# Who issues the store of a scan unit's step sizes and input maps, and when its first broadcast is loaded

## The chip, the cores and the metric

The kernel runs on one core of a Trainium2 chip. Time is device time of that core, in microseconds (us), from one launch to the end. The kernel before was run three times: 4187.68 us in the median (4182.67 to 4189.44). The engines are named PE (matrix multiply), DVE (vector), ACT (scalar, activations), POOL (GpSimd) and SP (which here only issues transfers).

## What is computed

Four layers in sequence work on x of shape (4, 512, 256). Layers 0, 1 and 3 are attention and feed-forward layers. The change lies in layer 2, a stack of four selective-scan blocks (Mamba blocks). Cut to what matters, one block is:

```
xi, z = split(rmsnorm(h) @ in_proj.T)
xi = silu(conv(xi) + conv_b)
dt, Bm, Cm = split(xi @ x_proj.T)                 # 16, 16 and 16 columns
dt = softplus(dt @ dt_proj.T + dt_b)
dA = exp(dt[..., None] * A)
dBu = dt[..., None] * Bm[:, :, None, :] * xi[..., None]
h_t = dA_t * h_(t-1) + dBu_t                      # a scan over time
y_t = sum_s(h_t * Cm_t) + xi * D
h = h + (y * silu(z)) @ out_proj.T
```

There are 512 inner features, 16 states for each of them, and 512 time steps after a prefix of 64 that is scanned earlier, beside layers 0 and 1.

## The kernel before

Layer 2 is cut into 16 units: 4 blocks times 4 batch elements, in that order. Inner features lie on partitions, in four chunks of 128; time lies along the free dimension. A unit is 32 steps: two pairs of chunks, and in each pair 8 pairs of states times 2 chunks. One step is a scan over 128 partitions of two states of 512 time steps each, 1024 elements in a row. The steps of all units are numbered through: step i belongs to unit i // 32.

A step runs over these instructions, each with its own tile rotation:

- `maps` (L1581): for every second step, SP loads two rows of B (tile bB, 3 buffers) and two rows of C (bC, 4 buffers) from a scratch tensor in DRAM, copied to all 128 partitions (512 KB each). The loads are issued four or five steps ahead.
- `decay` (L1596): ACT writes exp(dt * A) for the two states into PSUM (ps_dA, 2 buffers), one step ahead, so the tile of step i + 2 can be made once step i has been read.
- `product` (L1588): POOL multiplies dt * xi (dtx) with bB into dBu (4 buffers), two steps ahead in program order.
- `begin` (L1606): ACT puts the start value of the two scans into the first column of dBu.
- `states` (L1611): DVE runs the scan. In steps with i % 4 == 1 it writes to the tile hP in SBUF, in the others back to ps_dA.
- `outputs_here` (L1623) on DVE, or `outputs` (L1628) on POOL for the hP steps, multiply the states with bC: the output multiply.
- `add_up` (L1632): PE transposes and sums the result into ps_y, for all 16 states of a pair.

The rest of a unit is written as generators that are advanced twice a step, in a fixed order, until they give back control with `yield`. Every yield is therefore half a step. `front` (L1325) prepares the unit after next: the norm of h (hn), its projection (ps_in, copied to xp by ACT), the convolution as four matmuls (ps_cv, made xi by ACT), a Silu over all of xi (issued at fixed steps of the running unit), and then, on ACT, the tile xd (L1428) with the 16 step-size rows and the 32 rows of B and C. xd is stored to two scratch tensors in DRAM: scr0, the first column of B, and scr, all of B and C. Then the first column is loaded back as b0, on all partitions. `step` (L1444) waits for the mark "fronted" that front sets at its end, and makes dt and dtx of a pair of chunks: a matmul of xd with w_dt (ps_dt), an Identity activation with bias for each chunk (L1459), softplus over both (L1266), products, and the start values from b0. The Sqrt of the unit after that (L1366) is timed to follow softplus in the same half step, since each change of function table on ACT is an ACT_TABLE_LOAD. `close_pair` (L1662) and `gated` (L1506) take the sum of a finished pair (g, DVE) through the gate and the output projection.

Two things set the order around the change. The instructions of each engine stand in the order in which the program emits them, and each engine takes its own in that order. SP's queue holds the stores of xd (L1432, L1433), the load of b0 (L1439), the map loads (L1585) and the weight loads, in one sequence.

Of the kernel before, what the change touches and what calls it, by code (L numbers as in the profile page):

```python
# [29 lines left out]
NS = 16  # L30
R = 16
# [93 lines left out]
def kernel(ctx: ExitStack, tc: tile.TileContext, t: dict, out: bass.AP):  # L125
    nc = tc.nc
# [1141 lines left out]
    def layer2(hT, A, far, h63, tail, X, fw, wl, late):  # L1268
# [5 lines left out]
        with ExitStack() as st:  # L1274
# [50 lines left out]
            def front(n):  # L1325
# [101 lines left out]
                xd = q["xd"] = pool.tile([NX, T], F32, name="xd", tag="xd")  # L1427
                nc.scalar.copy(xd, ps[:NX, :])  # L1428
                done(ps)
                scr = q["scr"] = dram.tile([2, NS, T], F32, name="scr", tag="scr")  # L1430
                scr0 = dram.tile([NS, 1], F32, name="scr0", tag="scr0")
                nc.sync.dma_start(out=scr0, in_=xd[R : R + NS, 0:1])  # L1432
                nc.sync.dma_start(out=scr.rearrange("k s t -> (k s) t"), in_=xd[R:, :])  # L1433
                for _ in range(3):
                    yield
                while n and units[n - 1].get("used0") != EC:
                    yield
# [252 lines left out]
            with tc.manual_schedule():  # L1690
                for i in range(first, last):
                    n, r = divmod(i, US)
# [8 lines left out]
                    if i in (first, first + 8) or 0 <= n < NU - 2 and r == FS:  # L1701
                        active.append(front(0 if i == first else 1 if i < 0 else n + 2))
# [243 lines left out]
```

## Time and profile before

| | us |
|---|---|
| median of 3 runs | 4187.68 |
| lowest and highest | 4182.67, 4189.44 |
| profiled execution, its own time | 4180.73 |
| span of the profiled execution | 4178.8 |
| layer 2's scan steps, first to last scan | 1645.6 to 3450.7 |
| store of xd by SP, first and last | 1622.1 and 3267.7 |
| transfers bB and bC, issue to landing, median | 4.2 and 3.9 |
| store scr0 and store scr, issue to landing, median | 1.3 and 3.1 |
| load b0, issue to landing, median | 7.1 |

Busy time over the whole span is PE 3496.8, DVE 2992.9, POOL 2359.9 and ACT 2222.6 us. In the page's row of slices (40 equal parts of the span, each digit the busy tenths), the scan block is the stretch where DVE stands at 9:

```profile
PE   7998988988898797777888888888887667999789
...
DVE  5537456466545622999999999999999996766653
ACT  2345465455312724666666666666666553556332
POOL 2249259076100503989888988899988881000131
```

A line of the trace gives the start in us, the duration, the engine and the line of the program, the operation with its tiles, and in brackets how long the engine stood idle before it and which instruction's end is taken to have released it. "SPq" is SP's queue: the duration there is that of the issue, not of the transfer. A row of waits gives who waited for whom, the total in us, how often, and the longest. A wait for several instructions is put down to the one that came last.

### The profile page before, as it was taken

How to read it: one execution, taken by the hardware profiler on the slowest of the kernel's cores; microseconds unless marked ns; L12 is line 12 of the kernel's file. 1: busy time of each engine (PE TensorE's matmuls, PEld its weight loads, DVE VectorE, ACT ScalarE, POOL GpSimd, SP SyncE). 2: the span in 40 equal slices, each digit the busy share in tenths (PEclk: the TensorE clock that was granted, in tenths of full speed). 3: DMA queues.
4: the chain of work that ended last, by engine and by line, in shares of the span. 5: the costliest groups of instructions: out<-in, count | busy, mean ns of one | idle time of the engine just before them, and what ended most of it. 6: DMA issues, size and time to landing. Idle time of an engine off the chain costs nothing. (4 is left out here: it accounts for less than half of the span.)

```text
span 4178.8 us, 48666 instructions
## 1 busy us (share of the span) xinstructions
PE 3496.8 (84%) x17616; PEld 2207.9 (53%) x17616; DVE 2992.9 (72%) x2853; ACT 2222.6 (53%) x4475; POOL 2359.9 (56%) x1601
## 2 busy tenths in 40 slices
PE   7998988988898797777888888888887667999789
PEld 4654544545566363555555555555555444555446
DVE  5537456466545622999999999999999996766653
ACT  2345465455312724666666666666666553556332
POOL 2249259076100503989888988899988881000131
PEclk9999999999998898889888888888888778999999
DMA  2023022023100202444444444444444441000000
GB/s 75 11 85 102 23 79 94 17 95 94 42 1 1 77 7 78 162 152 158 148 161 152 150 156 159 150 143 151 167 159 140 149 141 36 1 1 1 1 6 16
DMA packets 140287, 369.93 MB, mean 89 GB/s; under 512 B 20624, under 2 KB 38224, under 8 KB 140048
## 3 DMA queue, kind: packets, MB, share of 16 engines
q1 hardware_dynamic: 137968, 364.63, 25.9%
q8 instruction: 139, 2.28, 0.2%
q10 hardware_dynamic: 2080, 2.20, 0.2%
q14 instruction: 100, 0.82, 0.1%
HBM read 363.50 MB, written 3.28 MB: 88 GB/s over the span
## 5 line engine op out<-in xcount | busy, mean ns | idle before, releaser
L1592 POOL TENSOR_TENSOR dBu<-dtx,bB 128x1022 f32<-128x1022 f32 x512 | 1198.2, 2360 | 92.4 <-DMA bB<-scr 47.3
L1619 DVE TENSOR_TENSOR_SCAN ps_dA<-ps_dA,dBu 128x1024 f32<-128x1024 f32 x384 | 878.0, 2286 | 125.6 <-POOL dBu L1592 98.6
L1604 ACT ACTIVATE ps_dA<-dt,A 128x512 f32<-128x512 f32 x1024 | 708.2, 692 | 440.5 <-DVE hC L1626 402.5
L1652 PE MATMUL ps_y<-ident,hC 128*128 128x128 f32 x3072 | 458.2, 304 | 52.4 <-DVE hC L1626 52.4
L1626 DVE TENSOR_TENSOR hC<-ps_dA,bC 128x1024 f32<-128x1024 f32 x384 | 470.0, 1224 | 24.5 <-issue 0.4
L1652 PEld LDWEIGHTS ps_y<-ident,hC 128*128 128x128 f32 x3072 | 410.3, 159 | 137.7 <-DVE hC L1626 73.7
L963 ACT ACTIVATE pr<-ps_s,nm 128x512 f32<-128x512 f32 x512 | 345.2, 686 | 258.3 <-DVE nm L959 258.3
L959 DVE TENSOR_REDUCE nm<-ps_s 128x2 f32<-128x1024 f32 x256 | 301.4, 1219 | 173.4 <-PE ps_s L948 156.8
L1630 POOL TENSOR_TENSOR hP<-hP,bC 128x1024 f32<-128x1024 f32 x128 | 301.9, 2359 | 77.2 <-issue 41.0
L977 PE MATMUL ps_pt<-ident,pr 128*128 128x128 f32 x2048 | 285.2, 279 | 62.8 <-DVE pT L982 37.4
L977 PEld LDWEIGHTS ps_pt<-ident,pr 128*128 128x128 f32 x2048 | 232.7, 142 | 162.9 <-issue 66.4
L1619 DVE TENSOR_TENSOR_SCAN hP<-ps_dA,dBu 128x1024 f32<-128x1024 f32 x128 | 291.7, 2279 | 0.0
L525 POOL TENSOR_TENSOR phb<-hT_res,pm 128x512 f32<-128x512 f32 x128 | 182.6, 1429 | 190.5 <-DMA pm<-scrp 146.0
L535 DVE TENSOR_TENSOR_SCAN phb<-pdA,phb 128x512 f32<-128x512 f32 x128 | 222.2, 1743 | 78.1 <-POOL phb L525 49.0
L178 PE MATMUL ps_cv<-xp,w_dg 128*128 128x512 f32 x512 | 238.7, 600 | 18.1 <-ACT dBu L1609 12.8
L1652 PE MATMUL ps_y<-ident,hP 128*128 128x128 f32 x1024 | 164.1, 313 | 101.7 <-POOL hP L1630 101.7
L996 PE MATMUL ps_o<-pT,V 128*64 128x256 f32 (+1 forms) x2048 | 221.4, 393 | 1.8 <-ACT AT L1014 1.8
L1652 PEld LDWEIGHTS ps_y<-ident,hP 128*128 128x128 f32 x1024 | 140.7, 164 | 144.4 <-POOL hP L1630 112.6
L982 DVE COPY pT<-ps_pt 128x512 f32<-128x512 f32 x256 | 164.8, 681 | 65.2 <-PE ps_pt L977 64.7
L948 PE MATMUL ps_s<-kT,qT 64*128 64x512 f32 (+1 forms) x1024 | 207.2, 643 | 1.5 <-DVE kT L1781 0.8
L980 ACT COPY pT<-ps_pt 128x512 f32<-128x512 f32 x256 | 139.9, 593 | 118.2 <-PE ps_pt L977 117.9
L1641 PE MATMUL ps_y<-w_dD,xi 128*128 128x128 f32 x512 | 113.8, 413 | 92.2 <-DVE g L1668 92.2
(272 smaller groups left out, 6190.0 us busy)
## 6 DMA issues: line engine op xcount, KB each, us to landing
bB<-scr SPq DMA_DIRECT2D x256, 512.0 KB, 4.2
bC<-scr SPq DMA_DIRECT2D x256, 512.0 KB, 3.9
pm<-scrp SPq DMA_DIRECT2D x224, 256.0 KB, 3.2
w_pw_in<-in_L_in SPq DMA_DIRECT2D x7, 512.0 KB, 4.6
X<-in_x SPq DMA_DIRECT2D x4, 512.0 KB, 7.3
w_L_W<-in_L_W SPq DMA_DIRECT2D x2, 1024.0 KB, 10.2
w_L_Wq<-in_L_Wq SPq DMA_DIRECT2D x2, 1024.0 KB, 4.9
w_L_Wo<-in_L_Wo SPq DMA_DIRECT2D x2, 1024.0 KB, 8.7
```

What stands on the lines that cost most here:

```text
L178: nc.tensor.matmul(dst, l, r, start=(i == 0), stop=(i == len(pairs) - 1))
L535: nc.vector.tensor_tensor_scan(hb, dA, hb, 0.0, ALU.mult, ALU.add)
L959: nc.vector.tensor_reduce(nm, ps, AX.X, ALU.max, negate=True)
L963: nc.scalar.activation(pr, ps[:, x, :], AF.Exp, bias=nm[:, x : x + 1], accum_out=rs[:, y : y + 1])
L977: nc.tensor.transpose(pp[:, t4, :], pr[:, t4 * P : (t4 + 1) * P], ident)
L996: nc.tensor.matmul(ps_o[0][j * stride : (j + 1) * stride, half * W2 : (half + 1) * W2], Vs[n][0][:, t4, h * stride : (h + 1) * stride], pT ...
L1592: nc.gpsimd.tensor_mul(dBu[:, :, 1:], dtx[:, 1:].unsqueeze(1).broadcast_to([P, 2, T - 1]), bmap[i // 2, 0][:, :, 1:])
L1604: nc.scalar.activation(dA, dt, AF.Exp, scale=A[:, l, m, s : s + 1])
L1619: nc.vector.tensor_tensor_scan(to, dA, dBus.pop(i).rearrange("p s t -> p (s t)"), 0.0, ALU.mult, ALU.add)
L1626: nc.vector.tensor_mul(hCs[i], dA, bmap[i // 2, 1])
L1630: nc.gpsimd.tensor_mul(hCs[i], hCs[i], bmap[i // 2, 1])
L1652: nc.tensor.matmul(y[:, j, k * P : (k + 1) * P], hC[:, s, j * P : (j + 1) * P], ident, is_transpose=True, start=False, stop=(2 * s2 + s == ...
```

## The change

The two stores of xd are issued by ACT, which makes xd, and no longer by SP; the large one (scr) goes first. The load of b0 stays on SP. From unit 2 on, `front` yields six times instead of three before it asks for b0, so b0 is loaded, and the unit marked as fronted, three yields later in the program's order. Units 0 and 1 keep three.

```
                 scr0 = dram.tile([NS, 1], F32, name="scr0", tag="scr0")
-                nc.sync.dma_start(out=scr0, in_=xd[R : R + NS, 0:1])
-                nc.sync.dma_start(out=scr.rearrange("k s t -> (k s) t"), in_=xd[R:, :])
-                for _ in range(3):
+
+                nc.scalar.dma_start(out=scr.rearrange("k s t -> (k s) t"), in_=xd[R:, :])
+                nc.scalar.dma_start(out=scr0, in_=xd[R : R + NS, 0:1])
+                for _ in range(6 if n > 1 else 3):
                     yield
                 while n and units[n - 1].get("used0") != EC:
                     yield
```

## The prediction

> **What bounds the kernel now.** I first read the page. DVE fills slices 16 to 32 of 40, about 1625 to 3440 us: the scan block. There the busy time of each engine in a stretch (us, then number of instructions) says:
>
> ```profile
> core 0: us, PE busy (x) PEld busy (x) DVE busy (x) ACT busy (x) POOL busy (x), PEclk, DMA share, GB/s
> 1690.00:3400.00 1710.00, 1365.50 (x6328) 932.28 (x6326) 1599.29 (x980) 1139.08 (x2088) 1541.99 (x920) 0.84 0.45 155
> ```
>
> DVE works 1599 of 1710 us (94%). The block can only gain from DVE's remaining idle time. Next I read who waited for whom (us in total, times, longest), first SP's queue, then the engines:
>
> ```profile
> SPq L1432 <- ACT xd L1428: 275.2, 16, 48.3
> ```
>
> ```profile
> DVE ps_dA L1619 <- POOL dBu L1592: 98.6, 21, 47.7
> POOL dBu L1592 <- DMA bB<-scr: 47.3, 12, 4.8
> DVE ps_dA L1619 <- ACT ps_dA L1604: 26.9, 27, 3.7
> DVE g L1668 <- PE ps_y L1652: 11.2, 9, 1.5
> ```
>
> SP stands before the store of xd, 15 us a unit, with the map loads behind it. POOL waits 47.3 us for late bB maps. But DVE never waits for a map, only for POOL (98.6, of which 47.7 is the block's start), ACT and PE. Whether POOL's 47.3 us become DVE's 98.6 is the main question, so I took one unit boundary in order of time, SP, then DVE, ACT and POOL:
>
> ```profile
> 2009.10 0.33 SPq L1585 DMA_DIRECT2D bC<-scr  x1
> 2024.84 0.32 SPq L1432 DMA_DIRECT2D scr<-xd  x1
> 2025.20 0.41 SPq L1433 DMA_DIRECT2D scr<-xd  x1
> 2025.71 0.37 SPq L1585 DMA_DIRECT2D bB<-scr  x1
> ```
>
> ```profile
> 2021.95 2.30 DVE L1619 TENSOR_TENSOR_SCAN ps_dA<-ps_dA,dBu 128x1024 f32<-128x1024 f32 x1 [3.17 <-POOL dBu L1592]
> ```
>
> ```profile
> 2015.40 1.93 ACT L1683 ACTIVATE xi<-xi 128x2048 f32<-128x2048 f32 x1
> 2017.22 1.89 ACT L1683 ACTIVATE zs<-zs 128x2048 f32<-128x2048 f32 x1
> 2019.14 1.28 ACT L1604 ACT_TABLE_LOAD   x1
> 2020.43 1.42 ACT L1604 ACTIVATE ps_dA<-dt,A 128x512 f32<-128x512 f32 x2
> ```
>
> ```profile
> 2024.33 2.36 POOL L1592 TENSOR_TENSOR dBu<-dtx,bB 128x1022 f32<-128x1022 f32 x1 [2.44 <-DVE ps_dA L1619]
> 2031.02 2.34 POOL L1592 TENSOR_TENSOR dBu<-dtx,bB 128x1022 f32<-128x1022 f32 x1 [4.33 <-DMA bB<-scr]
> ```
>
> DVE's 3.17 us wait is labelled POOL, and a product does end at 2021.89. But 107 scans had begun before 2021.95 and 111 products by then: this is scan 107 (counting from 0), and the product just ended is number 110. Scan 107's own product was done three products earlier. ACT's decay of scan 107 ends at 2021.85: ACT had been in the two Silu passes and their table loads since 2014.11. The wait is ACT's. The late map delays product 112 (2031.02), whose scan comes at 2038.14, nearly 5 us after that product ends. So the stall that the change removes lies in POOL's slack.
>
> **The change part by part.** Steps below are scan numbers; the order of instructions of the two programs gives the positions.
>
> (1) The stores leave SP: 16 x (0.32 + 0.41) = 11.7 us of issue and 275.2 us of standing. SP now passes bB 112, bC 112 and bB 114 before b0's load. bB 112 needs product 107 done (2012), lands about 4.2 us later (median row) and product 112 no longer waits: 4.3 us back for POOL, nothing for DVE. SP next stands at b0's load, which needs the small store landed: from about 2019.6 (product 109 done) to 2027 (store issued by 2025.7, 1.3 us to landing). Behind it stand bC 114, whose buffer comes free at 2025.6 anyway, and bB 116; they are read at 2047 and 2040.6, over 8 us after they land. b0 itself, 7.1 us to land, is read at 2050. Cost nothing; that cover is 8 us.
>
> The Trainium skill, "DMA: Bandwidth & Descriptors", section "Issuing engines are not separate DMA queues", speaks against the change: transfers issued by several engines share the same DMA engines, and another issuer saves only issue time. By that rule SP gains 11.7 us; by the waits row 275.2 + 11.7, since the move takes away a wait at the head of the queue. By either, DVE's time changes by nothing.
>
> (2) The stores enter ACT's queue, right after xd (2024.23, 0.57 us). The nearest rows are ACT's own issues of 64 to 128 KB rows, 0.33 to 0.59 us with one of 1.34. Two of 0.41 with gaps make 0.9 us; between 0.7 and 2.7. Their waits are for xd, just made, and for transfers long landed. Queued behind them is the decay of 109: it started at 2025.61 after 0.80 us idle and is needed at 2028.96, so it must start by 2027.5. At 0.9 us nothing is lost; at 2.7 us 0.1 us a unit. A gain is excluded, as ACT only gets more work. Value: 0.
>
> (3) Three more waits before b0 for units 2 to 15. The step-size work of the next unit's pair 0 then comes half a step later. On ACT the order was: decay 113, dt, decay 114, dt, table, softplus, table, sqrt, begin, table, decay 115. It becomes: decay 114, dt, begin, dt, table, softplus, table, sqrt, table, decay 115. So one dt leaves a gap where ACT idles and enters the one stretch where DVE already waits:
>
> ```profile
> 2040.25 0.69 ACT L1459 ACTIVATE dt<-ps_dt,cols 128x512 f32<-128x512 f32 x1 [0.47 <-PE ps_dt L1457]
> 2041.77 1.42 ACT L1604 ACTIVATE ps_dA<-dt,A 128x512 f32<-128x512 f32 x2 [0.83 <-DVE hC L1626]
> 2043.13 0.67 ACT L1459 ACTIVATE dt<-ps_dt,cols 128x512 f32<-128x512 f32 x1
> 2049.07 1.42 ACT L1604 ACTIVATE ps_dA<-dt,A 128x512 f32<-128x512 f32 x2
> ```
>
> ```profile
> 2050.59 2.30 DVE L1619 TENSOR_TENSOR_SCAN ps_dA<-ps_dA,dBu 128x1024 f32<-128x1024 f32 x1 [1.58 <-ACT ps_dA L1604]
> ```
>
> Decay 114 cannot start earlier: it waits until DVE's output multiply of step 112 has freed its PSUM buffer. From its start to decay 115's was 7.30 us; now 7.30 + 0.66 (a dt, start to next start, with begin overlapping). Scan 115 moves from 2050.59 to 2051.25: +0.66 us a unit. DVE's reciprocal and output multiply before it also move, inside that wait.
>
> (4) What comes back. From one Silu-delayed scan to the next is 112.09 us for units 2 to 4 but 112.51 on average for units 5 to 13: there the PE is late after standing for hP (4.38 us at 2148 in the first of them), so that ACT waits 1.99 us for the first step-size matmul and DVE 1.4 us for g. With POOL's hP 109 starting when scan 109 ends (2031.2, not 2033.3) and the second step-size matmul now behind y of step 111, both waits go, and these nine become 112.09 + 0.66 = 112.75: +0.24 each.
>
> Sum: 0.66 x 5 (units 2, 3, 4, 14, 15) + 0.24 x 9 = 3.3 + 2.2 = +5.5 us.
>
> (5) hn is scaled after scan 116 instead of before it (same DVE work), and the chain in, xp, cv, xi of the next unit comes about 3 us later. Walking it through with full-clock rows (in 1.9, xp 0.5, cv 3.67, xi 0.68): hn done 2058.4, xp 2061.8, cv 2062.4 to 2066.1, xi 2066.2, then decay 120 ends at 2068.2, against scan 120 at 2068.7. 0.5 us to spare; further on I find 0.7 to 1. Value 0; bounds 0 and the slower rival below (no gain: nothing there waits now). Silu comes at step 138, twelve after the last of xi, so xi is not late for it.
>
> The profiled execution took 4180.7 us (span 4178.8 and 1.9 outside); with +5.5 it would be 4186.2. The median of the runs is 7.0 above it, so the forecast is 4187.7 + 5.5 = 4193, with 4189 to 4199 for this case.
>
> **The rivals.** *Slower: ACT's convolution copies come too late.* ACT takes instructions in order, so xi of chunk 0, one step later, holds back decay 120. It decides once cv ends over 0.5 us later than worked out. The PE's clock can do that: after the 4.13 us gap ahead of rb it stayed at 0.50 from 2048 to about 2054, and that gap now grows to some 8 us. The skill's "TensorE: Matmul & The Clock Gate", Part 1, says that the clock is halved after an idle window of about 3.4 us and returns after as long a busy one. By that rule it is back by 2052 to 2055.5, by the row at about 2054.7, both before cv. One window later, cv takes 7.3 instead of 3.67 and DVE loses 3.2 us. With 1 us a unit on average: 5.5 + 14 = 19.5, 4207. For it: the thin slack. Against it: xi waits 1.4 us for cv already now and DVE loses nothing.
>
> *No net cost.* The PE waits go (9 x 0.42 = 3.8 us) and the extra dt finds cover, if DVE rather than ACT binds at scan 115: 4184. Against it: the 1.58 us wait, in all such units. The change not doing what it says, with SP standing at b0 instead, lands near 4188: here too.
>
> *Faster: the 3.17 us wait is POOL's after all* and comes from the standing queue: 15 x 3.17 = 47.5, 4140. Against it: the count of products, and that DVE starts 0.09 us after ACT's end each time.
>
> **How the numbers follow.** A measurement of this kernel can tell about 0.2% (8.4 us) from no change. Likeliest case 0.45 (0.35 within it, 0.10 beyond), slower rival 0.29, no net cost 0.17 (0.03 of it faster), faster rival 0.09. Faster 0.12, same 0.49, slower 0.39. The range 4180 to 4207 leaves out the faster rival and the slower rival's far half.
>
> **What would show it.** Right: SP's wait for xd gone and one at b0's load; POOL's wait for bB near 0; 3.17 us before the scan after Silu still there; the scan after softplus waiting about 2.2 us instead of 1.58 (from the start of scan 114's decay to the next decay 7.96), in all of units 2 to 14; g's wait for PE gone. Wrong: the 3.17 shrinks; new DVE waits for ACT five to eleven scans after softplus; or ACT's issues take over 2 us.

## The result and the profile after

The changed kernel took 4194.34 us in the median of 22 runs (4183.39 to 4203.06), the kernel before 4188.06 us in as many on the same chip (4178.67 to 4195.23). The ratio is 1.0016, with a 95% interval of 1.0008 to 1.0023: 6.3 us slower. With this many runs the interval excludes 1, although the difference is just below the 0.2% that I had named as the limit of a measurement. The median is 1.3 us from the forecast of 4193.

The profiled execution of the changed kernel has a span of 4197.8 us, 19.0 more than before. Most of that lies ahead of the scan steps: the first scan starts at 1657.98 instead of 1645.59, 12.4 us later. That stretch varies with the same code (in the second profile of the changed kernel, below, the first scan started at 1651.82), so I don't put it down to the change. A better measure is the time from the first to the last of the 512 scans: 1805.11 us before, 1810.98 after, 5.87 us more. I call it the block. It also repeats much better than the whole: a second profile of the changed kernel (below) gave 1810.98 again, although its span was 5.7 us shorter.

The same stretch of the profile after, in the columns of the table of busy times:

```profile
1690.00:3400.00 1710.00, 1348.55 (x6330) 903.79 (x6328) 1590.03 (x974) 1138.52 (x2086) 1540.38 (x918) 0.86 0.44 154
```

DVE (third pair) works 1590.0 us where it worked 1599.3: in equal time it did 974 instead of 980 instructions. DVE is still the engine that is nearly full, and it waits more.

Now SP's queue. Of the waits after (who waited for whom, total, times, longest), the one for xd is gone, and in its place stands the load of b0:

```profile
SPq L1440 <- DMA scr<-xd: 149.3, 16, 50.1
```

Around the unit boundary of the prediction, scans 106 to 109, SP's queue after reads:

```profile
2032.84 0.32 SPq L1586 DMA_DIRECT2D bB<-scr  x1
2039.91 0.32 SPq L1440 DMA_DIRECT2D b<-scr  x1
```

The second map now passes 7 us before b0 is asked for, and SP stands 6.75 us in between. So b0 comes later in the program's order but not in time: from unit 2 on it is asked for 4.7 us after the start of the Silu-delayed scan (2035.19 here), as in the kernel before, and it lands 8.6 to 10.1 us after that start instead of 11.6 to 12.2. POOL's wait for bB (47.3 us in 12 waits) no longer appears. And yet DVE's waits are these:

```profile
DVE ps_dA L1620 <- POOL dBu L1593: 92.0, 15, 47.7
...
DVE ps_dA L1620 <- ACT ps_dA L1605: 37.3, 33, 3.7
...
DVE rstd L1369 <- ACT rstd L1366: 15.6, 16, 1.1
```

Of the row with POOL's name, 47.7 us are the block's start; the rest are the waits before the scan after Silu, unchanged:

```profile
2035.19 2.30 DVE L1620 TENSOR_TENSOR_SCAN ps_dA<-ps_dA,dBu 128x1024 f32<-128x1024 f32 x1 [3.16 <-POOL dBu L1593]
```

The 6.6 us that this row lost only changed their name. They were six waits of 1.1 us before the scan after softplus (scan 115 and its like in other units). In each, the scan's own product had ended some 8 us earlier and its decay 0.10 us before it began, so they were ACT's too; the same scans now wait 1.49 us under ACT's name. The wait for ACT's decays therefore rose not by the 10.4 us from 26.9 to 37.3 but by about 4. The main growth stands before the reciprocal, 15.6 us; between 1690 and 3400 us it is 15.1, where it was 2.3 before. DVE's wait for PE before g (11.2 us in the same stretch) is gone. What ACT does before scan 115 is now:

```profile
2055.02 1.42 ACT L1605 ACTIVATE ps_dA<-dt,A 128x512 f32<-128x512 f32 x2 [1.99 <-DVE hC L1627]
2056.37 0.67 ACT L1460 ACTIVATE dt<-ps_dt,cols 128x512 f32<-128x512 f32 x1
...
2057.02 0.69 ACT L1460 ACTIVATE dt<-ps_dt,cols 128x512 f32<-128x512 f32 x1
...
2062.90 1.42 ACT L1605 ACTIVATE ps_dA<-dt,A 128x512 f32<-128x512 f32 x2
```

Both dt now lie behind decay 114, and from its start to decay 115's it is 7.88 us instead of 7.30. DVE's reciprocal before the change, then DVE in the same place after it:

```profile
2047.71 0.18 DVE L1369 RECIPROCAL rstd<-rstd 128x4 f32<-128x4 f32 x1 [0.43 <-ACT rstd L1366]
```

```profile
2061.62 0.18 DVE L1369 RECIPROCAL rstd<-rstd 128x4 f32<-128x4 f32 x1 [1.12 <-ACT rstd L1366]
...
2064.42 2.30 DVE L1620 TENSOR_TENSOR_SCAN ps_dA<-ps_dA,dBu 128x1024 f32<-128x1024 f32 x1 [1.49 <-ACT ps_dA L1605]
...
2072.52 2.28 DVE L1620 TENSOR_TENSOR_SCAN hP<-ps_dA,dBu 128x1024 f32<-128x1024 f32 x1
```

The reciprocal and scan 115 wait 1.12 + 1.49 = 2.61 us; in the kernel before they were 0.43 + 1.58 = 2.01 at this boundary (0.46 + 1.58 in others). That is the whole loss of a unit like 2 to 4, except that hn, which now stands behind scan 116 (at 2070.09), gives a little back, of which more below.

The period from one Silu-delayed scan to the next, listed by the unit whose step sizes are made in it, shows where the 5.87 us are:

| units | before, each | after, each | sum of the differences |
|---|---|---|---|
| 1 | 112.09 | 112.09 | 0 |
| 2 to 4 | 112.09 | 112.52 | +1.3 |
| 5 to 13 | 112.29 to 113.02 | 112.51 to 112.88 | +0.4 |
| 14 | 119.11 | 122.50 | +3.4 |
| 15 | 113.89 | 114.65 | +0.8 |

### The profile page after: what moved, and what is told of

The parts are those of the page before. It is cut to its first block, busy times and chain, and to the rows that moved or that the text cites. A ratio compares the mean times of both kernels' runs of the same rounds, so it can differ in the third digit from the quotient of the medians.

```text
span 4197.8 us, 48679 instructions
## 1 busy us (share of the span) xinstructions
PE 3491.6 (83%) x17616; PEld 2188.2 (52%) x17616; DVE 2993.3 (71%) x2853; ACT 2218.5 (53%) x4475; POOL 2362.3 (56%) x1601
## 5 line engine op out<-in xcount | busy, mean ns | idle before, releaser
L1653 PEld LDWEIGHTS ps_y<-ident,hC 128*128 128x128 f32 x3072 | 400.4, 157 | 156.0 <-DVE hC L1627 88.9
L178 PE MATMUL ps_cv<-xp,w_dg 128*128 128x512 f32 x512 | 240.0, 602 | 31.4 <-ACT xp L1403 15.6
L1653 PE MATMUL ps_y<-ident,hP 128*128 128x128 f32 x1024 | 152.7, 298 | 71.3 <-POOL hP L1631 71.3
L1653 PEld LDWEIGHTS ps_y<-ident,hP 128*128 128x128 f32 x1024 | 131.4, 155 | 103.8 <-POOL hP L1631 79.3
```

The costliest lines, as they stand in the source:

```text
L178: nc.tensor.matmul(dst, l, r, start=(i == 0), stop=(i == len(pairs) - 1))
L1653: nc.tensor.matmul(y[:, j, k * P : (k + 1) * P], hC[:, s, j * P : (j + 1) * P], ident, is_transpose=True, start=False, stop=(2 * s2 + s == ...
```

## The experiments

My theory: the stores on ACT are free and cure a lateness of PE, and the later dt costs. Rivals: ACT's issues themselves cost; SP's standing queue held DVE; b0's later place in SP's queue costs. "Block" is always the time from first to last scan in the run's profile.

**The two halves apart.** First the stores on ACT, with three yields everywhere (the diff is against the changed kernel, as are those below unless said):

```
-                for _ in range(6 if n > 1 else 3):
+                for _ in range(3):
```

> One half of the change alone: ACT issues the two stores of xd, and b0 is asked for after three yields in every unit, as before. My theory (the later dt costs, the stores on ACT are free, and the late PE of units 5 to 13 was SP's fault): from decay 114's start to decay 115's 7.30 us again, DVE's 3.16 us before the scan after Silu still there, the period between those scans 112.09 us in units 2 to 13; first to last scan 1805.1 - 9 x 0.42 = 1801.3 us, so 3.8 us under the kernel before (ratio 0.9991). Rival, ACT's two issues themselves cost: period 112.5, first to last scan 1806 or more. Rival, SP's standing queue was what held DVE: the 3.16 us shrinks, up to 47 us less.

Measured: block 1801.58 us, every period of units 1 to 13 112.08 or 112.09 except one of 112.44, the waits 0.46 + 1.58 and 3.16 as expected. The ratio to before was 0.9985 (0.9976 to 0.9995). So the stores on ACT alone are a small gain, and neither ACT's issues nor SP's standing is what the change paid for.

Then the later b0 alone, with the stores left on SP (against the kernel before):

```
                 nc.sync.dma_start(out=scr.rearrange("k s t -> (k s) t"), in_=xd[R:, :])
-                for _ in range(3):
+                for _ in range(6 if n > 1 else 3):
```

> The other half alone: SP issues the stores as before, and b0 is asked for six yields later from unit 2 on. My theory: from decay 114 to decay 115 7.88 us as after the change, period 112.52 us at least in units 2 to 4, and SP's standing (275 us) is back. The block from first to last scan is 1805.1 + 3 x 0.43 + 3.4 (unit 14) + 0.8 (unit 15) = 1810.6 us if the later dt also cures the late PE of units 5 to 13, and up to 1814.5 if only the stores on ACT cure it (9 x 0.43 more); I take 1812, 7 us over the kernel before (1.0017). Rival, the issues on ACT were the cost: 1805.

Measured: block 1819.31 us, ratio 1.0018 (1.0010 to 1.0026). The mechanism is as expected, the block 7 us longer than I took: most periods are 112.5, but four of them are 113.4 to 115.1. One of these shows the whole chain that the stores on SP set off, here as one line of POOL, PE, ACT and DVE each (scans 236 to 243):

```profile
2485.31 2.35 POOL L1592 TENSOR_TENSOR dBu<-dtx,bB 128x1022 f32<-128x1022 f32 x1 [4.96 <-DMA bB<-scr]
```

```profile
2490.01 1.97 PE L1652 MATMUL ps_y<-ident,hP 128*128 128x128 f32 x8 [6.17 <-POOL hP L1630]
```

```profile
2499.62 0.69 ACT L1459 ACTIVATE dt<-ps_dt,cols 128x512 f32<-128x512 f32 x1 [2.09 <-PE ps_dt L1457]
```

```profile
2504.23 0.18 DVE L1369 RECIPROCAL rstd<-rstd 128x4 f32<-128x4 f32 x1 [3.17 <-ACT rstd L1366]
```

A late map holds one product on POOL; the output multiply of the hP step stands behind that product; PE waits for hP; its matmuls then take about twice their usual time (1.97 us for eight instead of 1.04); the second step-size matmul comes late; ACT waits for it with decay 115 behind it; and DVE waits for ACT. So POOL's wait does reach DVE, but only by this way round. The two halves in one table:

| block, us | b0 after three yields | after six |
|---|---|---|
| stores on SP | 1805.11 | 1819.31 |
| stores on ACT | 1801.58 | 1810.98 |

The move to ACT is worth 3.5 or 8.3 us, the three extra yields cost 14.2 or 9.4. For the two kernels with the stores on ACT, the ratios of the whole runs given above agree with these blocks within their intervals. For the later b0 alone they do not: the runs show some 7 us over the kernel before, where the one profile has 14. So the 14.2 and the 8.3 rest on a single profile, and in the runs the whole change and the later b0 alone are about equal (1.0016 and 1.0018). The late maps may not come as often in each execution.

**Is it the late load or the late dt?** With five yields the load of b0 stands later in SP's queue, but ACT, PE, DVE and POOL have the same order of instructions as with three.

```
-                for _ in range(6 if n > 1 else 3):
+                for _ in range(5 if n > 1 else 3):
```

> ACT issues the stores, and b0 is asked for five yields later instead of six (unit 2 on): the instructions of ACT, PE and DVE then stand in the same order as with three, only SP's load of b0 and the products that read it come later. My theory, that the sixth yield costs because it moves a dt behind decay 114: equal to the kernel with the stores alone, period 112.09, first to last scan 1801.3 us, 3.8 under before. Rival, b0's later load itself costs (the start values come late): period 112.5, 1806 or more.

Measured: block 1801.63 us, ratio 0.9983 (0.9977 to 0.9990). The later place of the load costs nothing, and the trace says why: b0 is no later in time. With three, five and six yields SP stands at b0 until the small store has landed, and asks for it 4.7 to 4.9 us after the start of the Silu-delayed scan. What a load that really lands later would cost is thus not tested. The sixth yield alone costs 9.3 us of block, since with it the mark "fronted" comes after the half step in which pair 0 would have started, and the first dt falls behind decay 114.

**Whose are the 3.16 us?** The changed kernel without one of the two Silu passes:

```
                 q["hn_read"] = True
-                to_silu.append(zs)
```

> The changed kernel without the Silu of zs (the gate is left unactivated, so part of the computation is left out): ACT's stay in Silu before decay 107 is one pass of 1.85 us shorter, nothing of POOL or SP changes. My theory, that DVE's 3.16 us before the scan after Silu is ACT's although POOL's name stands on it: the wait falls to about 1.3 us in each unit, first to last scan from 1811.0 to 1783 us (15 x 1.85 less), ratio to before 0.995. Rival, POOL's product is what the scan waits for: 3.16 us stays, 1811 us.

Measured: block 1783.08 us, 27.9 less than after the change, ratio to before 0.9942 (0.9928 to 0.9955). The scan after Silu now reads:

```profile
2022.82 2.30 DVE L1619 TENSOR_TENSOR_SCAN ps_dA<-ps_dA,dBu 128x1024 f32<-128x1024 f32 x1 [1.37 <-ACT ps_dA L1604]
```

The wait shrank by 1.79 us, nearly a Silu pass (1.85), and the label itself went over to ACT. POOL's product was not what the scan waited for.

**What covers ACT's issues?** Eight, then three further small stores behind the two:

```
+                for k in range(8):
+                    scrx = dram.tile([NS, 1], F32, name="scrx", tag=f"scrx{k}")
+                    nc.scalar.dma_start(out=scrx, in_=xd[R : R + NS, 0:1])
```

> The changed kernel with eight more stores of one column of xd (64 bytes each row's worth, to scratch that nobody reads) issued by ACT after the two. Prices the cover of ACT's issues: decay 109 is next on ACT, and after the change it ends 1.86 us before scan 109 needs it, started by DVE's output multiply at 2038.92, right when the second issue ended. My theory: eight issues of 0.31 to 0.43 us make 2.5 to 3.4 us, of which 1.86 are covered; DVE gets a new wait of 0.6 to 1.6 us before scan 109, 14 units: first to last scan 1811.0 + 9 to 22, I take 1826 us, ratio to before 1.005. Rival, ACT's issues are hidden altogether: 1811. Rival, nothing of them was ever hidden: 1811 + 14 x 3 = 1853, and the two of the change would cost 10 us.

Measured: block 1885.19 us, 74 more than after the change, ratio to before 1.0210 (1.0194 to 1.0227). Dearer than any of my cases. ACT's queue with the issues and the decay behind them, at one boundary:

```profile
2063.26 6.82 ACTq L1437 DMA_DIRECT2D scrx<-xd  x8
2070.12 1.41 ACT L1608 ACTIVATE ps_dA<-dt,A 128x512 f32<-128x512 f32 x2 [7.72 <-DMA scrx<-xd]
```

The cover was as worked out: of these 6.82 us, DVE's scan 109 (at 2071.64) waited 5.00 for ACT, so 1.82 were hidden (1.86 expected). The price was not: the median of all such issues is 0.43 us, but single ones take up to 3.82 (2.41 and 1.36 at this boundary). In 13 of the 16 trains it is the eighth of the ten stores whose issue stands 3.1 us or more. The transfers back up as well: the first three land 1.4 to 2.3 us after their issue, the sixth to tenth mostly 5 to 10 us. At this boundary SP's issue of a map stood over the same stretch (2064.72 to 2067.26), so it is not ACT's queue alone that was held. What holds an issue so long stays open.

> The changed kernel with three more stores of one column of xd on ACT instead of eight. With eight, most issues took 0.43 us but single ones up to 3.8, 6.8 us in sum, and scan 109 waited 5.0. My theory: decay 109 has 1.82 us of cover (6.82 - 5.00), three issues of 0.43 make 1.3 and cost nothing: first to last scan 1811 us, no new wait at scan 109, so two issues of 0.8 us as in the change are covered too. Rival, also short trains stand at an issue (the long one comes at the third to fifth): up to 14 x 2 = 28 us more.

Measured with three: block 1810.97 us, no new wait, no issue above 0.53 us (though the fifth store lands 4.1 to 6.7 us after its issue); ratio to before 1.0016 (1.0009 to 1.0024), that of the change. Up to five issues are hidden, so the change's two are.

**Unit 14.** Its +3.4 us is not what the other units lose. In that period the final norm of the first batch element runs between the scans (`tokens`). After the change the four scalings of X stood in one stretch on DVE, in the kernel before in two. DVE before, then DVE and POOL after the change:

```profile
3198.51 2.02 DVE L1568 SCALAR_TENSOR_TENSOR X<-X,ss,row_l_fw 128x256 f32<-128x256 f32 x2
3202.65 2.94 DVE L1568 SCALAR_TENSOR_TENSOR X<-X,ss,row_l_fw 128x256 f32<-128x256 f32 x2
```

```profile
3215.89 7.26 DVE L1569 SCALAR_TENSOR_TENSOR X<-X,ss,row_l_fw 128x256 f32<-128x256 f32 x4
```

```profile
3219.94 2.53 POOL L1593 TENSOR_TENSOR dBu<-dtx,bB 128x1022 f32<-128x1022 f32 x1
```

The same operation on the last batch element, four scalings too, takes 1.67 us at 3490.70, when POOL is idle. Beside POOL's large multiplies, which follow each other without a gap here (they start at 3215.12, 3217.43 and 3219.94), they take four times as long, as much as three of those. Singly, a scaling takes either about 0.47 us or until 0.28 us after the end of one of POOL's instructions. After the change three of the four were held in this way (1.88, 2.57 and 2.56 us), before it two (1.62 and 2.56). The Trainium skill, "SBUF — State Buffer", section "SBUF: two separate sides", says that a DVE instruction with two inputs in SBUF and a GpSimd instruction that reads SBUF exclude each other, each for its whole length. The trace agrees: the scalings read X and the weights from SBUF, while hn, which reads one of its two large inputs from PSUM, keeps its 1.38 to 1.40 us. To see whether the stretch is the cost, I started these scalings one yield later, which puts a scan between the two halves again:

```
-                for _ in range(4 if b < B - 1 else 1):
+                for _ in range(5 if b == 0 else 4 if b < B - 1 else 1):
```

> The changed kernel, with the four scalings of X of batch element 0 (in unit 13) begun one yield later, so that a scan stands again between the first two and the last two. After the change they run in one stretch of 7.26 us, before it in two of 2.02 and 2.94. My theory, that 2.3 of the 3.4 us that the stretch from unit 13's to unit 14's Silu lost come from that: 122.5 falls to about 120.2, first to last scan 1811.0 - 2.3 = 1808.7 us. Rival, the scalings cost the same wherever they stand (they wait for POOL): 122.5 stays.

Measured: unit 14's period 120.25, block 1808.76 us, as expected; all other periods stayed. Two scalings were held again (4.37 us for the first pair) and two were free (0.85 us for the second). The ratio to before was 0.9993 (0.9984 to 1.0002), which is lower than a block 3.7 us longer than before should give; the rest lies outside the block, where nothing was edited, and I have no cause for it.

**The change once more.**

> The changed kernel once more, unaltered, for a second profile of it. If the time lies in the scan block as I read it, first to last scan is 1811.0 us again to about 0.3, whatever the whole span does; ratio to before 1.0015. If the block itself varied from run to run by several us, the comparisons of blocks above would mean little.

Measured: block 1810.98 us, each period the same to 0.02; ratio 1.0026 (1.0015 to 1.0037).

**A shorter stretch on ACT.** If the stretch from decay 114 to decay 115 sets the pace there, taking the table load and the Sqrt out of it must gain. On the kernel with the stores alone:

```
-                nc.scalar.activation(rstd, rstd, AF.Sqrt)
+                nc.gpsimd.tensor_tensor(rstd, rstd, mhalf[:, :TPB], ALU.pow)
                 yield
                 yield
-                nc.vector.reciprocal(rstd, rstd)
```

> Stores on ACT with three yields, and the root of hn's mean square is taken out of ACT's burst: POOL makes rstd by pow(-0.5), in place of ACT's table load and Sqrt and DVE's reciprocal. My theory, that the stretch from decay 114 to decay 115 on ACT bounds DVE at that place: it shrinks from 7.30 by 1.28 + 0.20 to 5.8 us, DVE's waits there (2.04 us) fall to about 0.6, 14 units x 1.45 = 20 us less than the stores alone: first to last scan 1781 us, ratio to before 0.994. Rival, POOL sets DVE's pace there: its pow (1.0 us by the row of the tokens' pow) delays the products, and the time stays at 1801 or rises by up to 14 us.

Measured: block 1808.71 us, ratio 1.0004 (0.9996 to 1.0012): no gain. The wait at scan 115 did fall, to 0.56 us, but in the stretch from 1690 to 3400 us DVE now waited 70 times for a decay, 40.1 us, instead of 31 times and 32.4 us in the kernel with the stores alone. Of the 70, 39 are new, 21.8 us in sum: three in each of 13 units, before scans 118, 120 and 122 and their like (the next expectation counts 56, with some that stood there already). PE had made rb earlier, then stood idle before the input projection:

```profile
2169.04 3.75 PE L185 MATMUL ps_in<-hn,w_inx 128*128 128x512 f32 x4 [5.34 <-DVE hn L1380]
```

The four took 3.75 us, where they take 1.96 in the kernel with the stores alone. xp came late, and ACT waited 2.89 us for it with a decay behind. This is the prediction's slower rival, which the change itself did not meet. So I moved hn forward as well, to one yield behind rb, on top of pow:

> POOL makes rstd by pow as before, and hn is scaled one yield after rb instead of three, which puts it between scan 114 and its output multiply. In the kernel with pow alone the input projection ran at half clock after a gap of 5.34 us on PE (3.75 instead of 1.96 us), the copy xp came late on ACT, and DVE got 56 small new waits for decays. My theory: with hn earlier the gap is cut, xp is ready in time, the small waits go, and the 1.45 us of the burst are kept: period 110.3 us, first to last scan about 1778 us, ratio to before 0.993. Rival, the pow on POOL is what costs (its 1.0 us delays hP or the products): 1805 us or more again.

Measured: block 1789.96 us, ratio 0.9943 (0.9930 to 0.9957). This version beats both kernels, by 0.57% of the time before (24 us, of which the block shows 15; I have no cause for the rest). What helped was not quite what I expected: the idle stretch of PE was hardly shorter (3.24 to 4.29 us), and the input projection still ran at half speed (3.60 to 3.75 us). But it began 6 us earlier, 26.1 instead of 32.1 us after the Silu-delayed scan, and DVE's waits before scans 118, 120 and 122 are gone in spite of that. The version missed the 1778 for two reasons: every second period is 111.4 instead of 110.3 (a decay standing behind xi, which waits for the convolution), and unit 14's is 123.9.

> As the kernel with pow and hn early, but hn two yields after rb instead of one: between scan 115 and its output multiply. With one yield every second unit lost 1.1 us (1.59 us wait for a decay that stood behind xi and its convolution on a half-clocked PE), 1790.0 us in all. My theory, that the time of the chain hn, in, xp, cv, xi against the decays decides: the input projection comes about 2.7 us later, closer to the kernel with pow alone (1808.7), so 1795 to 1805 us, ratio to before 0.997. Rival, only the place of hn among the scans matters (a scan's bubble is filled either way): 1790 or less.

Measured with two yields: block 1791.47 us, ratio 0.9974 (0.9965 to 0.9984). I had expected a longer time; in the block it is nearly as good, with periods of 110.4 and 111.7 mixed. The trace shows what sets them apart, here in the periods of units 5 (110.42 us) and 6 (111.76 us):

```profile
2173.24 1.95 PE L185 MATMUL ps_in<-hn,w_inx 128*128 128x512 f32 x4 [1.48 <-DVE hn L1379]
2283.67 3.28 PE L185 MATMUL ps_in<-hn,w_inx 128*128 128x512 f32 x4 [3.71 <-DVE hn L1379]
```

In all 13 periods of units 1 to 13 the projection starts 30.8 to 30.9 us after the Silu-delayed scan. In the five of 110.42 or 110.43 us it ran at full clock (1.95 or 1.96 us, granted clock 1.00). In the eight of 111.6 to 112.1 us it did not (2.37 to 3.65 us, clock 0.53 to 0.80), and the first convolution began 1.7 us later. No period departs from this, and the instructions are the same in all. So the time of the chain does decide, as I had expected. My estimate now, from these periods: with the slow clock in the other five units too, some 1.3 us more in each, the block would be about 1798 us, within the 1795 to 1805 that I had named. The idle stretch just before the projection does not tell by itself which clock it will get: 2.85 us went with full clock, 1.91 us with 0.63.

## Why the prediction was right, and which terms were off

**What bounds the kernel.** Right: the 3.16 us are ACT's, whatever name stands on them. Leaving out one Silu pass moved the wait by that pass. The six waits of 1.1 us under POOL's name were ACT's as well, so apart from the block's start nothing of the 98.6 us was POOL's.

**(1) Stores off SP.** Right in both parts: SP stands at b0 now, POOL's wait for bB is gone, and DVE gains nothing directly. SP's standing fell from 275.2 to 149.3 us, by much more than the 11.7 us of issue. The way by which it gains (late map, hP, PE, dt) was part of step 4, and the experiment with the late b0 alone shows it link by link.

**(2) Two issues on ACT.** Right: decay 109 still starts on DVE's release, and up to five issues cost nothing. The issue was 0.31 and 0.43 us. My cover of 1.9 us held to 0.1.

**(3) The later dt.** The mechanism was right, the term half as large again as it should be: +0.66 a unit was predicted, +0.43 measured in units 2 to 4. The stretch on ACT grew by 0.58 (7.88, not 7.96), and 0.15 came back from a place that I had set at nothing, hn in step 5. An output multiply starts 2.32 to 2.36 us after its own scan, an instruction that does not read that scan 2.20 us after it. After the change hn stands in that gap of scan 116. From the start of scan 115 to that of the hP scan 117 it is 8.25 us before (2050.59 to 2058.84) and 8.10 after (2064.42 to 2072.52). One sign of being right was misplaced: I had scan 115 wait about 2.2 us instead of 1.58, but it waits 1.49, and the growth stands before the reciprocal (1.12 instead of 0.43), which reads the Sqrt that the dt delays.

**(4) What comes back in units 5 to 13.** Right: the PE's lateness was worth 0.42 us a unit, and the stores on ACT alone recover it (block 3.5 us shorter against 3.8 predicted). The net was +0.4 us for the nine units instead of +2.2, since the 0.66 was 0.43. POOL's hP 109 and its like did start about 2 us earlier (9.4 us after the Silu-delayed scan instead of 11.4 to 11.7). PE's idle stretch before it shrank less, from 4.04 to 3.50 us at this boundary (2047.01), and the matmuls behind it still ran at half speed there (dt 2.07 us). ACT does not wait for them all the same. That both dt are asked for later is not needed for it: with the stores alone they are not, and ACT does not wait either.

**(5) hn and the chain to xi.** Cost 0, as predicted, with about 0.6 us to spare at scan 120. The pow kernels show that such slack is real and thin.

**Units 14 and 15.** I gave both +0.66. Unit 15 lost 0.76, unit 14 lost 3.39. This is the one step that failed outright: I took unit 14 for an ordinary unit, and had not looked at what else shares that period. There the half-step shift joined the scalings of X (7.26 - 2.02 - 2.94 = 2.30 us) and lengthened the waits before X's copies (1.70 - 0.63 - 0.29 = 0.78 us).

In sum, for units 2 to 4, 5 to 13, 14 and 15: predicted 2.0 + 2.2 + 0.66 + 0.66 = 5.5 us, measured 1.3 + 0.4 + 3.4 + 0.8 = 5.9. The sign, the place and the mechanism held. That the total came out so close is partly luck, since two errors cancelled: 2.5 us too much in units 2 to 13, 2.7 too little in unit 14.

## What to carry to other kernels

Where a scheduler counts in half steps, a delay has no proportional price: here five yields cost nothing and the sixth cost 9 us, because only the sixth moved an instruction into the stretch that DVE waits for. A load that is asked for later in the program need not be later in time, if its queue stands there anyway. So compare the order of instructions per engine first, and then ask of each that moved whether it left a gap or entered one. A wait carries the name of what ended last, so count which result the waiting instruction really reads before you shorten the named engine. And check the one unit that also hosts other work; a shift that costs 0.4 us elsewhere may cost 3 there.

## What the runs showed of the hardware that was not expected

- A train of issues on ACT is not priced by its single ones: ten in a row, median 0.43 us, had single ones of up to 3.82 us, mostly the eighth, and the last eight took 6.82 us at one boundary; with five in a row none was above 0.53.
- Four DVE scalings that read two tiles in SBUF took 1.67 us with POOL idle and 4.96 to 7.26 us beside POOL's products. Each one that was held ended 0.28 us after an instruction of POOL, so the price is counted in POOL's instructions: two or three of about 2.4 us.
- An idle PE costs the next matmuls even when it is not the bound: after 5.34 us the input projection took 3.75 instead of 1.96 us, and a gain of 1.5 us a unit on ACT was gone. In the last kernel the granted clock in that one projection separates the periods of 110.4 us from those of 111.6 to 112.1 us.
